# VectorE bound to the order of the source beside the attention units, and a pass's last maxima carried into the next pass

## The chip, the cores and the metric

The kernel runs on one core of one Trainium2 chip. The time is the device time of one execution in microseconds; the number compared is the median of the runs shown. The profile is one execution taken by the hardware profiler. Engine names: PE is TensorE, PEld its weight loads, DVE is VectorE, ACT is ScalarE, POOL is GpSimd, SP is SyncE, which issues most DMAs.

## The reference, cut to what matters

One layer over 512 query rows of width 512: cross attention to a context of 8192 rows with 16 heads of 64, then a state space block with an MLP, then a mixture of 16 experts. The change lies in the cross attention:

```python
q = (scale * (Q @ Wq + bq)).reshape(bs, q_len, NH, DM)   # Q = layernorm(x): 512 rows
k = (K @ Wk + bk).reshape(bs, kv_len, NH, DM)            # K = V = ctx_1024: 8192 rows
v = (V @ Wv + bv).reshape(bs, kv_len, NH, DM)
qk = jnp.einsum('nlhd,nshd->nhls', q, k)
a = jax.nn.softmax(qk, axis=-1)
o = jnp.einsum('nhls,nshd->nlhd', a, v).reshape(bs, q_len, NH * DM)
return o @ Wo + bo
```

The three stages after it are the same before and after the change; the kernel runs them in `tail`.

## The kernel before

Values are kept as pairs of 16-bit floats, a high and a low part, so that most products are three matmuls and most evictions from PSUM are two: ScalarE writes the high part, and VectorE subtracts to get the low part. The heads are taken in 8 pairs, the pairs in 4 passes of two. The context is cut into 16 chunks of 512 rows (`NCH`).

**The filler.** A generator, `filler`, makes keys, values and row maxima, pass by pass. For each chunk it runs two `kproj_units` (PSUM tile `psk`, evicted to `khl` by L257 and L258), two `vproj_units` (`psv`, evicted to `vs` by L280 and L281), and puts two `smax_units` on the list `side`. A unit of these computes plain scores (`psx`, L297), which ScalarE evicts to `sf` (L302) and VectorE folds into a running maximum `runm` (L308 for the first chunk, L310 after). `pump` takes one unit off `side`; it is called after every second projection unit (every fourth in pass 0). After the last chunk of a pass, a `while side` loop runs the rest of the maxima with no projections between. Then `maxrow_units` reduces `runm` (L317 twice, L318), TensorE transposes the result (`ptm`, L321), ScalarE writes it as a row (`mrow`, L323), and two DMAs place it in `qlm`, an operand of the real scores. Its first half runs at the end of the pass, its second inside the next pass's first chunk. `qproj` makes a pass's queries at its start (24 matmuls `psq`). `pass_weights` stages the next pass's weights through one staging buffer (L169), with the split on ScalarE (L175) and VectorE (L176) one chunk after the DMA is issued.

Each unit yields a planned cost in nanoseconds, and `advance` runs the filler until the sum of these costs has reached a given mark.

**The attention.** A unit is one pair and one half of the queries, and has 32 steps (`NSTEP`). In each step, `scores` runs 8 matmuls into two `pss` banks (L359, L360). ScalarE takes the exponential (L367, in even steps also L369), and VectorE casts (L371, odd steps) and subtracts (L372) to get `phl`. The value matmuls `av` (L389, L392) run two steps later, through the list `pend`. After a unit's last step `unit_end` normalises (L399 to L404) and transposes (`pto`, L410). Between a step's parts the loop calls `advance`, so that passes 1 to 3 of the filler are spread over the first `NFILL` = 380 steps at `rate` nanoseconds each. `LEAD` = 11500 ns of filler run before the first scores. Every second step also takes a turn of `weight_prep`, which loads later stages' weights (`mpf`, two buffers), splits them on VectorE (`mph`, L535 and L536) and stores them. The last unit runs beside the first part of `tail`.

**What sets the order.** TensorE's instructions, from pass 0 of the filler to the end of the unit before the last, are in the order of the source (`manual_schedule` with the set `PE`, L541). The other engines' order is chosen by a scheduler when the program is built, from a model of costs; each engine then executes its own list in that order, and waits where an operand is missing.

Of the kernel before, what the change touches and what calls it, by code (L numbers as in the profile page):

```python
# [8 lines left out]
F16 = mybir.dt.float16  # L9
# [7 lines left out]
P = 128  # L17
# [4 lines left out]
CH = 512  # L22
# [7 lines left out]
NPASS = NPAIR // 2  # L30
NDC = NCH // 2
HQ = NQ // 2
NSTEP = 32
PASSN = 16 * (4 * 2592 + 8 * 406) + 2 * 2592 + 600


@with_exitstack
def perceiver_layer(ctx: ExitStack, tc: tile.TileContext, a: dict, out: bass.AP):
# [78 lines left out]
    def R(es, name, bufs):  # L117
        return es.enter_context(tc.tile_pool(name=name, bufs=bufs, side="right", reuse_waits="tile"))
# [7 lines left out]
    def bank_j(shape, dtype, name):  # L126

        if jn[1]:
            jn[0] += 1
            if jn[0] % 3 == 0:  # L130
                return ps_o.tile(shape, dtype, name=name, tag="po1")
        return ps_j.tile(shape, dtype, name=name, tag="pj")
# [3 lines left out]
    sb2 = R(attn, "a2", 2)  # L136
# [30 lines left out]
    def stage_w(src, n, tag, stage=("wst", 1), bufs=2):  # L167
        st = sb2.tile([P, NC4, n], F32, name=f"wst_{tag}", tag=stage[0], bufs=stage[1])
        nc.sync.dma_start(st, src)  # L169
        return lambda: split_w(st, n, tag, bufs)  # L170
# [8 lines left out]
    def load_w(*x, **k):  # L179
        return stage_w(*x, **k)()  # L180
# [102 lines left out]
        nc.sync.dma_start(v_d[g][c // 2][:, tt : tt + 2], vs)  # L283
        yield 648

    def smax_units(c, qh, kh, runm, wide):

        for q2 in range(2):
            sf = sb3.tile([P, 2, 2, CH], F16, name="sf", bufs=2)
            pss = []  # L290
            for qi in range(2):
                qt = 2 * q2 + qi
                for hh in range(2):
                    s = slice(hh * 64, hh * 64 + 64)
                    pool, tag = (ps_s, "pss") if wide and qi else (ps_x, "px")
                    ps = pool.tile([P, CH], F32, name="psx", tag=tag)
                    nc.tensor.matmul(ps, lhsT=qh[s, qt * P : (qt + 1) * P], rhs=kh[s, 0, :], start=True, stop=True)  # L297
                    pss.append((sf[:, qi, hh, :], ps))
                if wide and not qi:
                    continue  # L300
                for dst, ps in pss:
                    nc.scalar.activation(dst, ps, AF.Copy, scale=1.0 / (8.0 * WS))  # L302
                pss = []
                if not qi:
                    yield 406
            r = runm[:, 2 * q2 : 2 * q2 + 2]
            if c == 0:
                nc.vector.tensor_copy(r, sf)  # L308
            else:
                nc.vector.tensor_tensor(r, r, sf, ALU.max)  # L310
            yield 626 if wide else 406

    def maxrow_units(p, runm):
        qlm = state[p]["q"][1]
        m = sb2.tile([P, 2, 4], F32, name="mx")
        for w in (256, 128):
            nc.vector.tensor_tensor(runm[:, :, :, 0:w], runm[:, :, :, 0:w], runm[:, :, :, w : 2 * w], ALU.max)  # L317
        nc.vector.tensor_reduce(m.rearrange("p h q -> p q h"), runm[:, :, :, 0:128], axis=AX.X, op=ALU.max)  # L318
        yield 0
        pt = bank_j([P, P], F32, "ptm")  # L320
        nc.tensor.transpose(pt[0:8, :], m.rearrange("p h q -> p (h q)"), ident)  # L321
        r = sb2.tile([8, P], F16, name="mrow")
        nc.scalar.activation(r, pt[0:8, :], AF.Copy, bias=PSHIFT, scale=-1.0)  # L323
        for hh in range(2):
            nc.sync.dma_start(
                qlm[64:65, hh, :].rearrange("o (a b) -> o a b", b=P), r[hh * 4 : hh * 4 + 4, :]
            )
        state[p]["ready"] = True
        yield 300
# [91 lines left out]
    def filler():  # L421
        side = []

        def pump():
            while side:
                u = next(side[0], None)
                if u is not None:
                    yield u
                    break
                side.pop(0)  # L430

        def pass_weights(g):
            pr = (2 * g, 2 * g + 1)
            out = []
            for src, n, tag, bufs in (
                (a["Wk"][pr[0]], P, "k", 4), (a["Wk"][pr[1]], P, "k", 4), (a["Wv"][g], 256, "v", 2),
                (a["Wq"][pr[0]], P, "q", 2), (a["Wq"][pr[1]], P, "q", 2),
            ):
                w = stage_w(src, n, tag, bufs=bufs)
                yield None  # L440
                out.append(w())
            yield out[0:2], out[2], out[3:5]

        mr, nw = [], None
        for g in range(NPASS):
            pr = (2 * g, 2 * g + 1)
            if g == 0:
                wk0 = load_w(a["Wk"][0], P, "k", bufs=4)
                nct = ctx_first(0)
                wk = [wk0, load_w(a["Wk"][1], P, "k", ("p32", 3), bufs=4)]  # L450
                wv = load_w(a["Wv"][0], 256, "v", ("p32", 3))
                nc.sync.dma_start(x_sb, a["x"])
                wq = [load_w(a["Wq"][p], P, "q", ("t2k", 4)) for p in pr]
            else:
                wk, wv, wq = nw
                qh = [qproj(p, w) for p, w in zip(pr, wq)]
                yield 2 * 2592
            runm = [sb2.tile([P, 4, 2, CH], F16, name=f"runm{i}", tag=f"runm{i}", bufs=1) for i in range(2)] if g else None
            ks = [[None] * NCH for _ in pr]
            for c in range(NCH):  # L460
                if c == NCH - 7 and g < NPASS - 1:
                    nws = pass_weights(g + 1)
                if c >= NCH - 7 and g < NPASS - 1:
                    nw = next(nws, None) or nw
                ct = nct
                nxt = g * NCH + c + 1
                if nxt < NPASS * NCH:
                    nct = ctx_first(nxt) if nxt < NCH else ctx_load(nxt % NCH)
                gens = [kproj_units(p, c, ct, wk[i], ks[i]) for i, p in enumerate(pr)]
                gens += [vproj_units(g, c, ct, wv, j) for j in range(2)]  # L470
                k = 0
                for n, gen in enumerate(gens):
                    for u in gen:
                        yield u
                        k += 1
                        if k % (2 if g else 4) == 0:
                            yield from pump()
                    if mr and c == 0:
                        yield from mr.pop(0)
                if g == 0 and c == 0:  # L480
                    first_norm()
                    qh = [qproj(p, w) for p, w in zip(pr, wq)]
                    yield 2 * 2592
                    runm = [sb2.tile([P, 4, 2, CH], F16, name=f"runm{i}", tag=f"runm{i}", bufs=1) for i in range(2)]
                if c == 2:
                    for p, q in zip(pr, qh):
                        qplace(p, *q)
                side += [smax_units(c, qh[i][0], ks[i][c], runm[i], g == 0) for i in range(2)]
            while side:
                yield from pump()  # L490
            mr = [maxrow_units(p, runm[i]) for i, p in enumerate(pr)]
            for x in mr:
                yield next(x)
            if g == NPASS - 1:
                for x in mr:
                    yield from x
            passes[0] = g + 1

    fill = filler()
    done = [0.0]  # L500

# [3 lines left out]
            done[0] = 1e12 if u is None else done[0] + u  # L505

    PE = {mybir.EngineType.PE}

    def weight_prep():
        zero = sb2.tile([P, 2 * DM], F16, name="zero", tag="t2k", bufs=4)  # L510
# [29 lines left out]
    ms = ExitStack()  # L540
    ms.enter_context(tc.manual_schedule(engines=PE))  # L541

    units = [(p, h) for p in range(NPAIR) for h in range(2)]
    NLAST = len(units) - 1
    LEAD = 11500
    loads = {}

    def load(j):
        if j < len(units) * NDC:
            loads[j] = main_load(units[j // NDC][0], j % NDC)  # L550
# [2 lines left out]
        advance(done[0] + 1)  # L553
    jn[1] = False
    start = done[0]
    load(0)
    advance(start + LEAD)
    load(1)
    pend, enders, early = [], [], weight_prep()
    NFILL = 12 * NSTEP - 4  # L560
    rate = (NPASS - 1) * PASSN / NFILL
    sp = (sb2, sb3, 3)
    po = []

# [10 lines left out]
    for n in range(NLAST * NSTEP):  # L575
# [3 lines left out]
        if m % 4 == 0 and n:  # L579
            load(n // 4 + 1)  # L580
        cur = scores(u, m, loads[n // 4], sp, n > NFILL)
        advance(start + LEAD + (n + 0.5) * rate)
        if enders and m == 4:
            for _ in enders.pop(0):
                pass
        while len(pend) > (2 if m == 2 else 1):
            drain()
        advance(start + LEAD + (n + 1.0) * rate)
        pend.append((u, m, cur))
        if n < NFILL and n % 2 == 0:  # L590
            next(early, None)
# [4 lines left out]
    while enders:  # L596
        for _ in enders.pop(0):
            pass
    attn.close()
    ms.close()  # L600
    late2 = R(late, "late2", 1)
    sp = (late2, late2, 3)
# [756 lines left out]
```

## Time and profile before

| what | us |
|---|---|
| median of 3 runs | 2649.29 (2645.43 to 2654.56) |
| profiled execution, device time | 2653.45 |
| its span, first to last instruction | 2651.7 |
| TensorE busy | 2410.6 |
| VectorE busy | 2049.4 |
| ScalarE busy | 1955.5 |
| mean granted TensorE clock | 0.959 |

Pass 0 of the filler runs alone until about 265 us; attention and filler run together from about 280 to 1625 us; attention alone to about 1810 us; the last unit with the beginning of the tail to about 1915 us; then the tail. Lines such as L372 are line numbers of the kernel before. Matmuls overlap, and their ends are modelled, so TensorE's busy time is more than the time its matmuls need; the distance between their starts and the granted clock tell more.

### The profile page before, as it was taken

To read this page: it belongs to the slowest core of one execution; us is meant where nothing else is said; L and a number is where in the kernel's file an instruction comes from. 1 tells how busy PE (TensorE), PEld (TensorE's weight loads), DVE (VectorE), ACT (ScalarE), POOL (GpSimd) and SP (SyncE) were. 2 spreads that over 40 slices of the span, in tenths; PEclk is the share of its full clock that TensorE was granted. 3 is DMA by queue.
4 is the path that set the end of the run, shared out by engine and by line. 5 is a ranking of instruction groups with operands and counts; after the bars stand their busy time and mean duration, and the time that the engine had idled before them with its cause. 6 is when DMAs were issued, how large, how long until landed. Compare 5 with 4: busy or idle time off the path is not lost. (4 is left out here: it accounts for less than half of the span.)

```text
span 2651.7 us, 54346 instructions
## 1 busy us (share of the span) xinstructions
PE 2410.6 (91%) x21806; PEld 1693.5 (64%) x21806; DVE 2049.4 (77%) x2403; ACT 1955.5 (74%) x3734; POOL 44.2 (2%) x58
## 2 busy tenths in 40 slices
PE   7999998999999899998999998998878688998895
PEld 4454676777666677766677766997656466665442
DVE  6876688877877877777877777997899999633785
ACT  5787787888787788867788887997868476432784
POOL 2000000000000000000000000000000000001001
PEclk9999999999899999989999998999989889999998
DMA  7973899866598866658966655887511322675896
GB/s 265 308 255 128 268 284 270 242 169 187 166 268 264 265 189 176 184 152 250 253 176 190 173 162 129 201 204 206 171 56 41 96 72 82 229 233 200 294 337 222
DMA packets 353686, 531.42 MB, mean 200 GB/s; under 512 B 25106, under 2 KB 218834, under 8 KB 353300
## 3 DMA queue, kind: packets, MB, share of 16 engines
q1 hardware_dynamic: 352148, 523.69, 65.6%
q0 software_dynamic: 1280, 4.20, 0.5%
q8 instruction: 173, 2.83, 0.5%
q14 instruction: 85, 0.70, 0.1%
HBM read 397.68 MB, written 126.94 MB: 198 GB/s over the span
## 5 line engine op out<-in xcount | busy, mean ns | idle before, releaser
L372 DVE TENSOR_TENSOR phl<-p,phl 128x1024 f16<-128x1024 f32 x512 | 625.9, 1224 | 175.0 <-ACT phl L369 158.9
L367 ACT ACTIVATE p<-pss 128x512 f32<-128x512 f32 x1024 | 596.8, 619 | 126.1 <-PE pss L360 50.7
L302 ACT ACTIVATE sf<-psx 128x512 f16<-128x512 f32 x1024 | 557.7, 622 | 79.1 <-PE psx L297 77.2
L359 PE MATMUL pss<-qhh,k 128*128 128x256 f16 x2048 | 486.2, 277 | 18.5 <-ACT phl L369 18.0
L360 PE MATMUL pss<-qlm,kb 128*128 128x256 f16 x2048 | 485.2, 276 | 0.6 <-DMA kb<-k_d 0.4
L389 PE MATMUL po<-v,phl 128*128 128x130 f16 x4096 | 327.2, 222 | 5.2 <-DVE oq L402 4.7
L310 DVE TENSOR_TENSOR runm<-runm,sf 128x2048 f16<-128x2048 f16 x240 | 292.4, 1218 | 45.7 <-ACT sf L302 45.2
L389 PEld LDWEIGHTS <-phl 128*128 128x128 f16 x4096 | 273.9, 99 | 69.4 <-issue 21.5
L369 ACT ACTIVATE phl<-pss 128x512 f16<-128x512 f32 x512 | 312.3, 610 | 0.0
L274 PE MATMUL psv<-wh_v,ctxc 128*128 128x256 f16 x1024 | 283.4, 277 | 7.7 <-DVE khl L258 3.4
L275 PE MATMUL psv<-wl_v,ctxc 128*128 128x256 f16 x1024 | 282.2, 276 | 1.2 <-DVE wl_v L176 1.2
L276 PE MATMUL psv<-wh_v,ctxc 128*128 128x256 f16 x1024 | 282.1, 276 | 0.0
L359 PEld LDWEIGHTS <-k 128*128 128x128 f16 x2048 | 202.2, 99 | 63.7 <-issue 18.0
L360 PEld LDWEIGHTS <-kb 128*128 128x128 f16 x2048 | 202.7, 99 | 61.0 <-issue 22.2
L297 PE MATMUL psx<-khl,qh 64*128 64x512 f16 x1024 | 212.5, 395 | 21.3 <-ACT sf L302 18.4
L371 DVE CAST phl<-p 128x1024 f16<-128x1024 f32 x256 | 176.1, 688 | 58.1 <-ACT p L367 57.7
L392 PE MATMUL po<-v,phl 128*128 128x65 f16 x4096 | 209.9, 194 | 9.3 <-DVE phl L372 9.3
L250 PE MATMUL psk<-ctxc,wh_k 128*128 128x512 f16 x512 | 198.6, 388 | 21.1 <-DVE vs L281 10.5
L919 PE MATMUL py<-hs,ident 128*128 128x256 f32 x512 | 148.1, 447 | 67.1 <-DVE hs L916 67.0
L251 PE MATMUL psk<-ctxc,wh_k 128*128 128x512 f16 x512 | 197.2, 385 | 0.7 <-DVE ctxc L234 0.7
L252 PE MATMUL psk<-ctxc,wl_k 128*128 128x512 f16 x512 | 196.8, 384 | 0.0
L392 PEld LDWEIGHTS <-phl 128*128 128x128 f16 x4096 | 172.8, 98 | 12.8 <-DVE phl L372 12.0
(304 smaller groups left out, 3711.9 us busy)
## 6 DMA issues: line engine op xcount, KB each, us to landing
v<-v_d SPq DMA_DIRECT2D x128, 520.0 KB, 4.4
k<-k_d SPq DMA_DIRECT2D x256, 256.0 KB, 5.8
ctxc<-ctx_d SPq DMA_DIRECT2D x96, 512.0 KB, 5.2
wef<-in_gu_dram SPq DMA_DIRECT2D x72, 512.0 KB, 5.9
v_d<-vs SPq DMA_DIRECT2D x128, 260.0 KB, 3.8
k_d<-khl SPq DMA_DIRECT2D x128, 256.0 KB, 4.2
kb<-k_d SPq DMA_DIRECT2D x128, 256.0 KB, 5.4
wpm<-w_d SPq DMA_DIRECT2D x48, 512.0 KB, 3.9
```

The lines of the kernel that those rows point to most:

```text
L274: nc.tensor.matmul(ps[:, t, :], lhsT=ct[i // 2][:, 0, i % 2, sl], rhs=wh[:, i, :], start=i == 0, stop=False)
L275: nc.tensor.matmul(ps[:, t, :], lhsT=ct[i // 2][:, 0, i % 2, sl], rhs=wl[:, i, :], start=False, stop=False)
L276: nc.tensor.matmul(ps[:, t, :], lhsT=ct[i // 2][:, 1, i % 2, sl], rhs=wh[:, i, :], start=False, stop=i == NC4 - 1)
L302: nc.scalar.activation(dst, ps, AF.Copy, scale=1.0 / (8.0 * WS))
L310: nc.vector.tensor_tensor(r, r, sf, ALU.max)
L359: nc.tensor.matmul(ps[:, hh], lhsT=k[:, hh, sl], rhs=qhh[:, hh, qs], start=True, stop=False)
L360: nc.tensor.matmul(ps[:, hh], lhsT=b[:, hh, sl], rhs=qlm[:, hh, qs], start=False, stop=True)
L367: nc.scalar.activation(p32[:, i], pss[i], AF.Exp, scale=sc)
L369: nc.scalar.activation(ph[:, i], pss[i], AF.Exp, scale=sc)
L372: nc.vector.tensor_tensor(pl, p32, ph, ALU.subtract)
L389: nc.tensor.matmul(o, lhsT=ph[:, i, hh, qs], rhs=vv, start=first, stop=False, **kw)
L392: nc.tensor.matmul(o, lhsT=pl[:, i, hh, qs], rhs=vv_, start=False, stop=last, **kw)
```

## The change

VectorE is added to the engines that keep the order of the source, and this begins where the filler's first pass has been made, ahead of the first loads of keys; until there TensorE alone keeps it, as before. ScalarE, SyncE and GpSimd keep the scheduler's order. The loop at the end of a pass goes, except in the last pass. The last chunk's maxima stay on `side`, the two `maxrow_units` are put behind them, and both run inside the next pass's first chunks, with a pump after every projection unit as long as `side` holds more than two. `maxrow_units` has three turns of no planned cost between the reduce and the transpose. `runm` is made when the first chunk's maxima run. In the last pass, every unit of the rest has 800 ns of planned cost added (`LAST / 10`). `LEAD` goes from 11500 to 27500, `NFILL` from 380 to 378, and `rate` takes both into account.

```diff
+LAST = 8000
...
-    def smax_units(c, qh, kh, runm, wide):
+    def smax_units(c, i, qh, kh, runm, wide):
+        if c == 0:
+            runm[i] = sb2.tile([P, 4, 2, CH], F16, name=f"runm{i}", tag=f"runm{i}", bufs=1)
...
-            r = runm[:, 2 * q2 : 2 * q2 + 2]
+            r = runm[i][:, 2 * q2 : 2 * q2 + 2]
...
-    def maxrow_units(p, runm):
+    def maxrow_units(p, i, runm):
+        runm = runm[i]
...
-        yield 0
+        for _ in range(3):
+            yield 0
...
-                        if k % (2 if g else 4) == 0:
+                        if k % (2 if g else 4) == 0 or len(side) > 2:
                             yield from pump()
-                    if mr and c == 0:
-                        yield from mr.pop(0)
...
-                side += [smax_units(c, qh[i][0], ks[i][c], runm[i], g == 0) for i in range(2)]
-            while side:
-                yield from pump()
-            mr = [maxrow_units(p, runm[i]) for i, p in enumerate(pr)]
-            for x in mr:
-                yield next(x)
+                side += [smax_units(c, i, qh[i][0], ks[i][c], runm, g == 0) for i in range(2)]
+            side += [maxrow_units(p, i, runm) for i, p in enumerate(pr)]
             if g == NPASS - 1:
-                for x in mr:
-                    yield from x
+                while side:
+                    yield from pump()
+                    yield LAST / 10
...
     PE = {mybir.EngineType.PE}
+    ALL = PE | {mybir.EngineType.DVE}
...
-    LEAD = 11500
+    LEAD = 27500
...
     start = done[0]
+    ma = ExitStack()
+    ma.enter_context(tc.manual_schedule(engines=ALL))
     load(0)
...
-    NFILL = 12 * NSTEP - 4
-    rate = (NPASS - 1) * PASSN / NFILL
+    NFILL = 12 * NSTEP - 6
+    rate = ((NPASS - 1) * PASSN + LAST - LEAD) / NFILL
...
     attn.close()
+    ma.close()
     ms.close()
```

More of the change, by code (lines that the diff above doesn't have):

```diff
@@ L442, in pass_weights @@
             yield out[0:2], out[2], out[3:5]
-        mr, nw = [], None
+        nw = None
         for g in range(NPASS):
@@ L457, in filler @@
                 yield 2 * 2592
-            runm = [sb2.tile([P, 4, 2, CH], F16, name=f"runm{i}", tag=f"runm{i}", bufs=1) for i in range(2)] if g else None
+            runm = [None, None]
             ks = [[None] * NCH for _ in pr]
@@ L483, in filler @@
                     yield 2 * 2592
-                    runm = [sb2.tile([P, 4, 2, CH], F16, name=f"runm{i}", tag=f"runm{i}", bufs=1) for i in range(2)]
                 if c == 2:
```

## The prediction

> **What bounds the kernel now.** I read the page first, its busy times and its 40 slices:
>
> ```profile
> PE 2410.6 (91%) x21806; PEld 1693.5 (64%) x21806; DVE 2049.4 (77%) x2403; ACT 1955.5 (74%) x3734; POOL 44.2 (2%) x58
> ...
> PE   7999998999999899998999998998878688998895
> ...
> PEclk9999999999899999989999998999989889999998
> ```
>
> TensorE is the busiest, and its dents stand beside dents of its granted clock. So I then cut the attention stage (240 to 1650 us) into a table of stretches; columns are busy us and instruction count per engine, the granted clock, DMA share and GB/s.
>
> ```profile
> 395.00:425.00 30.00, 23.52 (x217) 16.07 (x215) 23.70 (x38) 17.19 (x35) 0.00 (x0) 0.83 0.87 259
> 675.00:705.00 30.00, 25.57 (x185) 14.08 (x183) 24.28 (x26) 21.27 (x41) 0.00 (x0) 0.77 0.37 109
> 855.00:890.00 35.00, 26.15 (x253) 18.63 (x251) 27.73 (x43) 19.92 (x41) 0.00 (x0) 0.90 0.81 254
> 1600.00:1650.00 50.00, 40.71 (x435) 30.63 (x434) 38.68 (x38) 37.30 (x74) 2.19 (x5) 0.83 0.43 108
> 900.00:1140.00 240.00, 239.91 (x2519) 174.37 (x2517) 182.47 (x202) 204.51 (x402) 0.00 (x0) 1.00 0.68 191
> ```
>
> The last row is the stage undisturbed: TensorE full, clock 1.00, 10.50 matmuls per us, about 3.36 us per attention step (it holds 72 of the subtracts L372, one a step). Nothing but TensorE's own work bounds it, and the change leaves that work as it is. The other rows are holes, of two kinds.
>
> First kind: a weight split (mph, L535) at the head of VectorE's queue, waiting for its DMA. The timeline of VectorE, then of TensorE:
>
> ```profile
> 398.99 0.74 DVE L258 SCALAR_TENSOR_TENSOR khl<-psk,bk_sb,khl 128x512 f16<-128x512 f32 x1
> 403.17 0.76 DVE L535 TENSOR_SCALAR mph<-mpf 128x512 f16<-128x512 f32 x2 [3.44 <-DMA mpf<-in_outp_dram]
> ...
> 409.06 0.68 DVE L281 TENSOR_TENSOR vs<-psv,vs 128x512 f16<-128x512 f32 x1
> ```
>
> ```profile
> 409.80 0.69 PE L410 MATMUL pto<-ident,oq 128*128 128x128 f32 x2 [6.47 <-DVE vs L281]
> ```
>
> The vs eviction that frees TensorE's PSUM bank stands behind the waiting split and behind what piled up, and TensorE idles 6.47 us. The waits of 260 to 1560 us show it as a class (total, times, longest):
>
> ```profile
> PE psk L250 <- DVE vs L281: 10.5, 2, 6.7
> PE pto L410 <- DVE vs L281: 10.2, 3, 6.5
> ```
>
> ```profile
> DVE phl L372 <- ACT phl L369: 134.4, 110, 3.7
> DVE phl L371 <- ACT p L367: 54.4, 73, 2.9
> DVE mph L535 <- DMA mpf<-in_w_dram: 24.2, 12, 5.4
> DVE mph L535 <- DMA mpf<-in_Wo_dram: 11.1, 4, 4.4
> DVE mph L535 <- DMA mpf<-in_rsu_dram: 10.8, 3, 5.7
> ```
>
> Second kind: at each pass's end the loop drains its last maxima alone. The timeline of TensorE at 680 us:
>
> ```profile
> 679.77 0.27 PE L359 MATMUL pss<-qhh,k 128*128 128x256 f16 x1
> 679.88 0.27 PE L360 MATMUL pss<-qlm,kb 128*128 128x256 f16 x1
> ...
> 682.20 0.86 PE L297 MATMUL psx<-khl,qh 64*128 64x512 f16 x2 [1.08 <-ACT sf L302]
> ...
> 685.18 1.07 PE L297 MATMUL psx<-khl,qh 64*128 64x512 f16 x2 [0.99 <-ACT sf L302]
> 686.18 0.40 PE L359 MATMUL pss<-qhh,k 128*128 128x256 f16 x1
> ...
> 689.86 1.07 PE L297 MATMUL psx<-khl,qh 64*128 64x512 f16 x2 [1.25 <-ACT sf L302]
> ```
>
> Each psx pair waits for ScalarE's evictions, the clock goes to half, and the scores, which started every 0.11 us at 679.8, are recorded at 0.40.
>
> [...] The clock: from the rows, the stretch 675 to 705 has a granted clock of 0.77, and no recorded wait there is over 1.3 us. [...] I take the row: many short gaps cost the clock too.
>
> [...] But in 900 to 1140 us weight loads are at 174/240 = 73% and 256-column matmuls start back to back every 0.11 us; there is no more to be had from TensorE there. [...]
>
> **Size of the holes.** First kind, by missing matmuls at 10.50 per us: 395-425: (315 - 217)/10.5 = 9.3 us. In the same way 745-760 (124 matmuls) 3.2, 795-830 (288) 7.6, 855-890 10.9, 1205-1240 (261) 10.1, 1265-1315 (463) 5.9: together 47 us. Second kind, idle plus clock loss: 240-280 (busy 37.15, clock 0.87) 2.9 + 5.2 = 8; 675-705: 11; 1140-1175 (30.80, 0.80) 4.2 + 7.0 = 11; 1600-1650: 9.3 + 8.5 = 18: together 48 us. So 95 us can be had at most.
>
> **The change, part by part.**
>
> *Source order on VectorE.* In the source a mpf fetch is issued four steps of the preparation ahead of its split, one every two attention steps: 8 x 3.36 = 27 us, against waits of at most 5.7 us. In the built order the fetches on SP stand about every 12 instructions instead of in bunches, and the splits one pair at a time among the attention steps. The 57 us of VectorE waits on mpf should go, and with them the 47 us. Residue for late stores or loads on SP: 5 us.
>
> What it adds: VectorE now stands where something is late. Its work is the same, 77%. The built order of ScalarE follows TensorE's in both kernels, so VectorE's operations become ready in about the order they stand in. Behind a waiting subtract (L372) queue khl, vs and running maxima; waiting for those are TensorE's next psk/psv bank (two banks, a group every 6.5 us: four per chunk, eight steps per chunk) and the av matmuls, which run two steps after their scores (pend). A lag of some 4 us is covered; the waits in the rows are 134.4/110 = 1.2 us. Bounds: 0, and the rival below; I take 6 us.
>
> *Next pass's weights.* Split by ScalarE (L175) then VectorE (L176), now one per chunk, on one staging buffer: a DMA starts when the split before it is done, and ScalarE's half stands only about three steps later. In the trace the longest such wait of ScalarE is 6.29 us (wh_q at 815 us), 12.4 us in all. Bounds 0 and 12; I take 6.
>
> *Drain removed.* An eviction costs ScalarE 0.51 us (four sf in a row take 2.05 in its timeline), a psx pair TensorE about 0.21. Pass 0: four last units of four evictions (2.05 us of ScalarE) each beside one kproj unit: 2.05 + 0.16 of ScalarE against 0.65 + 0.85 of TensorE, 0.7 us each, 3 us. Passes 1 and 2: each half unit gives ScalarE 1.02 us beside a 0.65 us projection; at 1.67 of them a step (1.76 us of planned filler over 0.648 + 0.406) ScalarE needs 1.70 + 3 x 0.51 + 0.25 = 3.5 us against TensorE's 3.36, 1 us over five steps. The maxrow operations (1.22 + 0.69 + 1.22 us, twice a pass) are a lump in VectorE's order, mostly inside its lag: 2 us. So 3 us per pass, 6. The four pumps between reduce and transpose hide the reduce. Last pass: with 800 ns added per unit there are 1.43 half units a step, ScalarE 1.53 + 1.46 = 3.0 us against TensorE's 2.2 us (1.6 a step without filler, 1650 to 1810 us: 2356 matmuls, 24 a step; and 0.6): 0.8 x 5.6 steps = 4.5, with the maxima 6 us. Together 15 us of the 48 stay.
>
> *LEAD, LAST, NFILL.* The same filler, 16 us of it ahead of the first scores: 0, as TensorE is full in both places. The maxima's rows (two qlm DMAs each) go out later, behind the zero fills and ahead of the first k loads on SP; the longer lead covers them. The last ones come about six steps before the unit that needs them: some 10 us against a 4 us landing. POOL's order is unchanged.
>
> **Sum.** 95 - 5 - 6 - 6 - 15 = 63 us. From the profiled execution's 2653.45: 2590; its time is 4.2 us over the median, so on the scale of the median 2649.29 - 63 = 2586.
>
> **Rivals.** (1) *All comes back*: no new waits, a residue of 10 us: 2564. For it: undisturbed stretches of 240 us exist. Against it: ScalarE at 85% there leaves little room at the pass ends.
> (2) *Half comes back*: ScalarE, whose order stays the scheduler's, takes the weight waits at full price (12), every maxima lump falls on TensorE (8 x 2.9 = 23), and short gaps keep costing the clock: gain some 30, 2620.
> (3) *Slower: VectorE becomes the bound.* It is free for about 23% of a 3.36 us step, 0.75 us. If waits in its fixed order pass that per step, every step grows. Now 110 of some 390 steps wait 1.2 us; if all did, 0.45 us over, times 378 steps = 170 us, less the 63 gained: 107 slower; at 1.05 us a step, 0.30 x 378 = 113, or 50 slower: 2700. It decides from 0.92 us a step. Against it: the order of ScalarE agrees with VectorE's new one.
> (4) *The order is not what bound*, holes elsewhere take their place: no change, 2649.
>
> **How the numbers follow.** Case of the sum 0.56 (2572 to 2604), (1) 0.12, (2) 0.14, (4) 0.05, (3) 0.13. A change within 0.3%, 8 us, cannot be told from none. Faster 0.82, same 0.05, slower 0.13. The range 2558 to 2641 takes in (2) and most of (1), and leaves (3), (4) out.
>
> **What would show it.** Right: no mph wait on mpf over 2 us; no clock below 0.9 in a 30 us stretch between 300 and 1560 us; VectorE still near 2049 us busy; the tail from the end of attention as long as now. Wrong: psk, psv or po waiting on VectorE in every step, with L372 waits in most steps (rival 3); sf or wh waits with half clock at the pass ends (rival 2).

## The result, and the profile after

The changed kernel takes 2610.67 us (median, 2607.52 to 2615.35, four runs) against 2649.67 us for the kernel before, measured beside it: ratio 0.9854, 95% interval 0.9831 to 0.9877, or 39 us faster. The forecast was 2586 us, a gain of 63. The direction and the first half of the mechanism were right; the gain was 24 us too high.

The page of the profile after, with its busy times and two rows of its slices (TensorE and its granted clock):

```profile
PE 2392.4 (92%) x21806; PEld 1684.3 (64%) x21806; DVE 2063.4 (79%) x2403; ACT 1948.3 (75%) x3734; POOL 44.3 (2%) x58
...
PE   7999899999999999999999998998877688998995
...
PEclk9999999999999999999999999999989899999997
```

The dents that the clock row of before has in its first 25 slices are gone at this resolution. The attention stage in stretches (columns as before: length, busy us and count of TensorE, weight loads, VectorE, ScalarE, GpSimd; clock, DMA share, GB/s):

```profile
395.00:425.00 30.00, 30.00 (x320) 21.61 (x317) 26.46 (x38) 25.34 (x53) 0.00 (x0) 1.00 0.74 213
...
855.00:890.00 35.00, 34.45 (x352) 24.47 (x351) 29.62 (x39) 29.34 (x60) 0.00 (x0) 1.00 0.80 230
...
1145.00:1180.00 35.00, 29.96 (x282) 21.49 (x280) 26.93 (x32) 20.52 (x42) 0.00 (x0) 0.90 0.68 183
1200.00:1540.00 340.00, 337.00 (x3539) 246.59 (x3536) 273.61 (x319) 287.34 (x568) 0.00 (x0) 1.00 0.73 209
1560.00:1610.00 50.00, 40.98 (x468) 32.49 (x466) 39.09 (x40) 37.74 (x76) 2.65 (x5) 0.90 0.44 118
```

The holes of the first kind (395, 855) are full, and 340 us run on end at 10.4 matmuls per us, against 10.50 in the undisturbed stretch before. What is left stands at the pass ends: 1145 to 1180, and above all the last one, 1560 to 1610, idle for 9.0 of its 50 us, where 1600 to 1650 had 9.3 before, at a clock of 0.90 instead of 0.83. TensorE's waits from 260 to 1560 us, total, times, longest:

```profile
PE psx L300 <- ACT sf L305: 7.4, 10, 2.5
PE ptm L326 <- DVE vs L282: 6.0, 3, 2.7
PE ptm L326 <- DVE mx L322: 4.2, 2, 2.6
PE ptm L326 <- DVE khl L259: 3.2, 1, 3.2
```

Three of the four are new: TensorE at the transpose of the maxima (`ptm`). And VectorE's own waits in the same stretch:

```profile
DVE phl L377 <- ACT phl L374: 165.4, 167, 2.7
DVE phl L376 <- ACT p L372: 32.8, 45, 1.9
DVE vs L282 <- ACT vs L281: 14.4, 19, 3.1
```

No `mph` wait is in that list any more. (The lines of the kernel after are shifted: L377 is L372 of before, L322 is L318, L326 is L321, L282 is L281, L259 is L258, L305 is L302.)

To place gains in time, the next table gives the start of the n-th attention step in each trace, as the difference in us to the same step before (278.5 us for step 0, 506.3, 1205.3, 1548.0, 1809.8 and 2651.7 for the end). (Left out of it: steps 32, 128 and 384, told below where they matter.) The changed kernel puts 16 us more filler ahead of step 0, which comes back by step 378. The last column is the median time of the runs; the kernel before had a median of 2649.6 to 2650.4 each time. A trace is one of the runs and need not be the median one: that of the order alone without the last maxima is the fastest of its five (2568.66 us).

| kernel | step 0 | 64 | 256 | 352 | 480 | end | median us |
|---|---|---|---|---|---|---|---|
| changed kernel | +14.8 | +4.2 | -22.0 | -39.1 | -41.7 | -38.0 | 2610.67 |
| order alone | -1.0 | -12.6 | -22.5 | -38.7 | -34.8 | -35.4 | 2618.28 |
| carrying alone | +12.8 | +13.8 | -12.4 | -27.2 | -32.0 | -34.5 | 2621.86 |
| before, no load waits | +4.4 | +1.7 | -15.8 | -26.0 | -25.1 | -22.7 | 2630.05 |
| carrying alone, no load waits | +10.4 | +2.3 | -33.4 | -46.5 | -49.9 | -53.0 | 2601.93 |
| changed, eight turns | +9.6 | -1.6 | -35.6 | -47.8 | -52.0 | -52.4 | 2602.14 |
| order alone, last maxima left out | -13.8 | -25.4 | -54.2 | -69.9 | -81.8 | -84.7 | 2575.45 |
| changed, eight turns, last maxima left out | +8.6 | +1.1 | -30.2 | -46.9 | -66.7 | -69.2 | 2586.58 |

All kernels in the table have their gain by step 480; the tail gives or takes a few us at most.

### The profile page after: what moved, and what is told of

Same layout as the page of the kernel before. It is cut to its first block, busy times and chain, and to the rows that moved or that the text cites. A ratio compares the mean times of both kernels' runs of the same rounds, so it can differ in the third digit from the quotient of the medians.

```text
span 2613.6 us, 54412 instructions
## 1 busy us (share of the span) xinstructions
PE 2392.4 (92%) x21806; PEld 1684.3 (64%) x21806; DVE 2063.4 (79%) x2403; ACT 1948.3 (75%) x3734; POOL 44.3 (2%) x58
## 5 line engine op out<-in xcount | busy, mean ns | idle before, releaser
L377 DVE TENSOR_TENSOR phl<-p,phl 128x1024 f16<-128x1024 f32 x512 | 626.7, 1225 | 189.4 <-ACT phl L374 177.6
L372 ACT ACTIVATE p<-pss 128x512 f32<-128x512 f32 x1024 | 597.8, 621 | 113.4 <-issue 41.9
L305 ACT ACTIVATE sf<-psx 128x512 f16<-128x512 f32 x1024 | 559.1, 627 | 69.2 <-PE psx L300 68.6
L364 PE MATMUL pss<-qhh,k 128*128 128x256 f16 x2048 | 482.7, 275 | 15.0 <-ACT phl L374 12.4
L394 PEld LDWEIGHTS <-phl 128*128 128x128 f16 x4096 | 271.8, 98 | 61.7 <-issue 14.6
L922 PEld LDWEIGHTS py<-hs,ident 128*128 128x128 f32 x512 | 107.8, 219 | 105.5 <-DVE hs L919 85.2
```

The lines of the kernel that those rows point to most:

```text
L364: nc.tensor.matmul(ps[:, hh], lhsT=k[:, hh, sl], rhs=qhh[:, hh, qs], start=True, stop=False)
L372: nc.scalar.activation(p32[:, i], pss[i], AF.Exp, scale=sc)
L377: nc.vector.tensor_tensor(pl, p32, ph, ALU.subtract)
L394: nc.tensor.matmul(o, lhsT=ph[:, i, hh, qs], rhs=vv, start=first, stop=False, **kw)
L922: nc.tensor.matmul(py[:, j, :], lhsT=ident, rhs=hs[:, n, 1:], start=k == 0, stop=False)
```

## The experiments

**One half of the change at a time.** First the order alone, on the kernel before:

```diff
     PE = {mybir.EngineType.PE}
+    ALL = PE | {mybir.EngineType.DVE}
...
     start = done[0]
+    ma = ExitStack()
+    ma.enter_context(tc.manual_schedule(engines=ALL))
...
     attn.close()
+    ma.close()
```

> The kernel before with one part of the change: VectorE keeps the order of the source from the same point on; the pass ends, LEAD, NFILL and the rate are those of before. Theory (two separate gains: the order takes away the holes behind waiting weight splits, the carry those at the pass ends): no mph wait on mpf over 2 us, the drains at 250, 680, 1150 and 1600 us stay at half clock, gain about 30 us, 2620. Rival A (the carry alone brings the gain): within 8 us of 2649. Rival B (the order is only of use together with the carry): slower than 2657.

Measured: 2618.28 us (2617.37 to 2621.67), ratio 0.9885 (0.9864 to 0.9906). No `mph` wait is left. From step 288 to 352, where nothing disturbs either kernel, before takes 216.4 us and this one 216.5: the fixed order of VectorE costs nothing there. The pass ends are as empty as they were: from 240 to 280 us TensorE is busy for 37.15 us at a granted clock of 0.87 in both kernels, and at 684.55 us the scores start every 0.21 us, as from 686.18 us on before.

Then carrying alone: the changed kernel with VectorE left to the scheduler.

```diff
-    ALL = PE | {mybir.EngineType.DVE}
+    ALL = PE
```

> The changed kernel with VectorE's order given back to the scheduler: carry, LEAD, LAST and NFILL stay. Theory (two separate gains): the mph waits on mpf are back (some 50 us of VectorE), the long half-clock stretches at the pass ends are not; gain about 12 to 17 us, 2635. Rival A (the carry alone brings the gain): about 2611, as the whole change. Rival B (order and carry only work together): 2649 or slower.

Measured: 2621.86 us (2618.87 to 2624.81), ratio 0.9898 (0.9879 to 0.9917): 28 us, well over the 12 to 17 expected. The load waits are there (VectorE's waits, 250 to 1560 us):

```profile
DVE mph L535 <- DMA mpf<-in_w_dram: 21.4, 13, 4.0
DVE mph L535 <- DMA mpf<-in_outp_dram: 9.0, 3, 3.6
DVE mph L535 <- DMA mpf<-in_rsd_dram: 5.0, 3, 2.0
DVE mph L535 <- DMA mpf<-in_inp_dram: 4.7, 2, 3.0
```

So the order gives 31 us and carrying 28, but together they give 39, not 59. Twenty us had to be found.

**The load waits by themselves.** On the kernel before, `mpf` is fetched once and used for all blocks, so that no split has a load to wait for (later stages get wrong weights):

```diff
+        kept = []
         def fetch(j):
+            if kept:
+                return kept[0]
...
+            kept.append(f)
             return f
```

> The kernel before, with the weight preparation fetching only its first block and splitting it again and again: every later mpf fetch is left out, so the stages after attention get wrong weights. VectorE's operations and the stores stay, the scheduler still orders VectorE. Theory (the first kind of hole is the wait for the DMA at the head of VectorE's queue): nearly all of the 47 us come back though no order is kept, about 2605 to 2612. Rival (the hole is the bunching of the splits ahead of vs and the subtracts, the wait only a part): under half, 2630 or more.

Measured: 2630.05 us (2628.88 to 2631.03), ratio 0.9925 (0.9901 to 0.9950): 20 us, where the rival begins (2630 or more): the wait is only a part of the hole. Two thirds of what the order gives by step 352 (26.0 of 38.7) come with the waits. What is left is the built order, which stays, with its bunched splits and the waits for stores that come in. Of VectorE's waits here and of TensorE's timeline, one line each:

```profile
DVE mph L540 <- DMA w_d<-mph: 6.8, 5, 2.8
```

```profile
413.36 0.44 PE L410 MATMUL pto<-ident,oq 128*128 128x128 f32 x2 [3.75 <-DVE vs L281]
```

The splits now wait in part for the store of their buffer's last content, and the hole at 400 us remains although nothing waits for a load: from 403.4 to 413 us VectorE works without a pause, and the eviction stands behind its splits and subtracts. Steps 32 to 64, which hold that hole, take 119.3 us before, 116.3 here, 108.4 with the order alone, 111.1 with carrying alone, 106.8 with both. Each half closes most of it, and it can only be closed once: 10.9 and 8.2 us apart, 12.5 together, so about 7 of the 20 us.

The same edit on carrying alone:

> The version that carries the maxima but leaves VectorE to the scheduler (2621.86 us), with mpf fetched once and used for every block, so that the splits have no load to wait for; later stages get wrong weights by it. Carrying alone gained 28 us and the order alone 31, but both together 39. If that is because the version with carrying alone has lost part of the first kind already (its built order is another one, and TensorE's longest waits for VectorE are 3.4 and 5.4 us instead of 6.7 and 6.5), taking the load waits away gives it no more than 11 us, down to about 2611 us or above. If the waits still cost it what they cost the kernel before (20 us), it comes to about 2602 us, below the changed kernel, and the two gains overlap for some other reason.

Measured: 2601.93 us (2595.65 to 2609.45), ratio 0.9820 (0.9793 to 0.9847). The 11 us I expected at most were wrong: the load waits cost this version the same 20 us as before, and 20 + 28 add up to the 48 measured. So load waits and carrying look independent, within the scatter of this run. And this kernel, with the scheduler's order, beats the changed kernel by 9 us: the source order must bring a cost of its own once the maxima are carried.

**What the order costs at the pass ends.** The timeline of VectorE after, at the end of the third pass, then that of TensorE:

```profile
1153.37 1.94 DVE L321 TENSOR_TENSOR runm<-runm 128x2048 f16<-128x2048 f16 x2
1155.35 1.22 DVE L322 TENSOR_REDUCE mx<-runm 128x8 f32<-128x1024 f16 x1
1156.48 0.68 DVE L376 CAST phl<-p 128x1024 f16<-128x1024 f32 x1
1157.20 1.23 DVE L377 TENSOR_TENSOR phl<-p,phl 128x1024 f16<-128x1024 f32 x1
1158.34 0.68 DVE L282 TENSOR_TENSOR vs<-psv,vs 128x512 f16<-128x512 f32 x1
...
1166.78 1.95 DVE L321 TENSOR_TENSOR runm<-runm 128x2048 f16<-128x2048 f16 x2
1168.76 1.22 DVE L322 TENSOR_REDUCE mx<-runm 128x8 f32<-128x1024 f16 x1
```

```profile
1159.08 0.27 PE L326 MATMUL ptm<-ident,mx 128*8 128x128 f32 x1 [2.39 <-DVE vs L282]
...
1170.04 0.31 PE L326 MATMUL ptm<-ident,mx 128*8 128x128 f32 x1 [2.65 <-DVE mx L322]
```

The folds and the reduce are 3.2 us in one piece. The first transpose waits for the eviction behind them, which frees its bank; the second waits for the reduce itself. The six transposes up to 1560 us wait 13.4 us in all (the three rows of `ptm` above), the last pass's two another 5.7 (two of the recorded texts below say 15.9 for the six). In the version with carrying alone the waits of the six are at most 1.7 us each. Putting more turns between reduce and transpose tests it:

```diff
-        for _ in range(3):
+        for _ in range(8):
             yield 0
```

> The changed kernel with eight turns of no planned cost between reduce and transpose in maxrow_units instead of three. Theory (the transposes ptm come too early: in the trace of the change they stand 1.7 to 3.8 us for mx or for an eviction queued behind the reduces, six of them 15.9 us in all): these waits go in passes 1 and 2 and shrink in the last, gain 8 to 14 us on the change, about 2599. Rival (the reduces are a lump in VectorE's order, and the next psk or psv bank waits for the same lump instead): within 4 us of 2611.

Measured: 2602.14 us (2600.16 to 2604.86), ratio 0.9823 (0.9801 to 0.9844). It beats both kernels, the changed one by 8.5 us. The transpose's waits, 260 to 1560 us, are down to:

```profile
PE ptm L326 <- DVE vs L282: 1.7, 2, 1.2
```

The mean granted clock from 240 to 1650 us says the same. The rows of the kernel before, of the changed kernel and of this one, in this order:

```profile
240.00:1650.00 1410.00, 1347.76 (x13577) 961.85 (x13576) 1085.71 (x1299) 1126.26 (x2202) 2.29 (x6) 0.97 0.72 208
```

```profile
240.00:1650.00 1410.00, 1368.21 (x14196) 990.97 (x14195) 1136.81 (x1346) 1159.20 (x2282) 2.75 (x6) 0.99 0.74 215
```

```profile
240.00:1650.00 1410.00, 1371.88 (x14359) 996.77 (x14358) 1146.76 (x1355) 1170.38 (x2304) 2.75 (x6) 1.00 0.74 216
```

**Four variants of that version, none of them better.** ScalarE kept to the source order too:

```diff
-    ALL = PE | {mybir.EngineType.DVE}
+    ALL = PE | {mybir.EngineType.DVE, mybir.EngineType.Activation}
```

> The kernel with eight turns, and ScalarE put into the order of the source as well. Theory (ScalarE's built order already follows TensorE's, so binding it changes next to nothing; only the waits of wh on its weight DMA, 5.6 us in the trace of the change, may go): within 5 us of that kernel's 2602, rather below. Rival (the scattered holes of some 20 us between 500 and 1450 us come from ScalarE being placed by the scheduler's model): 2590 or less. Rival (in the source a split or an eviction stands where ScalarE must wait): 2610 or more.

2601.47 us (2595.50 to 2606.20): no difference. The last pass's last maxima put on the list after two projection units of its last chunk, instead of after the chunk:

```diff
+                last = g == NPASS - 1 and c == NCH - 1
...
+                    if last and n == 2:
+                        side += [smax_units(c, i, qh[i][0], ks[i][c], runm, g == 0) for i in range(2)]
...
-                        if k % (2 if g else 4) == 0 or len(side) > 2:
+                        if k % (2 if g else 4) == 0 or len(side) > 2 or last:
...
-                side += [smax_units(c, i, qh[i][0], ks[i][c], runm, g == 0) for i in range(2)]
+                if not last:
+                    side += [smax_units(c, i, qh[i][0], ks[i][c], runm, g == 0) for i in range(2)]
```

> The kernel with eight turns; in the last pass alone, the last chunk's smax units are put on the list after its two kproj units and taken after every vproj unit, so that they run beside projections and not beside attention alone. Theory (the last pass's end is bound by ScalarE: eight half units of 1.02 us in steps in which ScalarE has 1.53 of 1.6 us used): gain 5 to 8 us on 2602, about 2596, and the hole at 1560 to 1600 us goes. Rival (the maxima rows and their reduces set that end): within 3 us of 2602.

2603.19 us (2600.66 to 2606.00): no gain. The last scores ended 6 us sooner, and steps 384 and 480 stood where they had. The reduce cut into pieces, with a turn after each fold and six turns after it:

```diff
         for w in (256, 128):
             nc.vector.tensor_tensor(runm[:, :, :, 0:w], runm[:, :, :, 0:w], runm[:, :, :, w : 2 * w], ALU.max)
+            yield 0
...
-        for _ in range(8):
+        for _ in range(6):
```

> The kernel with eight turns, and a turn after each of the two folds in maxrow_units (six turns after the reduce), so that the 3.2 us lump of VectorE becomes three pieces of 1.2 us at most with subtracts between. Theory (with the transposes moved away the lump is covered by the two-step slack of the value matmuls and the banks): gain under 4 us, 2600. Rival (the lump still stops a bank's eviction at each pass end): gain 6 to 10 us, 2594.

2602.95 us (2597.40 to 2605.18): nothing. And both of these together:

> Last maxima early and reduce in pieces together. Theory: the sum of the two gains, about 2594. Rival (both give back the same wait): no better than the better one.

2602.18 us (2600.11 to 2603.45): no gain in the time. In its profile, though, step 480 stands at -58.0, 6 us ahead of the eight turns alone, and the tail gives it back (848.7 us from step 480 to the end instead of 841.4). Why the tail is longer was not tried.

**What the drains were worth.** In three kernels the maxima of each pass's last chunk are left out, so that a pass ends with none to make, only with the reduce and the transposes: the order alone, the changed kernel, and the changed kernel with eight turns.

```diff
-                side += [smax_units(c, i, qh[i][0], ks[i][c], runm, g == 0) for i in range(2)]
+                if c < NCH - 1:
+                    side += [smax_units(c, i, qh[i][0], ks[i][c], runm, g == 0) for i in range(2)]
```

What falls away with them is eight units of eight matmuls, 32 pairs (the first text below counts them too high, its 14 us are right). Their own price is read in an undisturbed stretch of the timeline before:

```profile
906.70 0.27 PE L275 MATMUL psv<-wl_v,ctxc 128*128 128x256 f16 x1
906.81 0.27 PE L276 MATMUL psv<-wh_v,ctxc 128*128 128x256 f16 x1
907.01 0.39 PE L297 MATMUL psx<-khl,qh 64*128 64x512 f16 x2
907.34 0.63 PE L389 MATMUL po<-v,phl 128*128 128x130 f16 x8
```

From the last `psv` to the `po` behind the pair it is 0.53 us instead of the 0.11 us from one `psv` to the next, so a pair costs 0.42 us, and 32 of them 13.4 us. (That is 0.21 us for 512 columns over 64 rows; three `psk` matmuls of 512 columns over 128 rows take 0.65 us there, from 911.36 to 912.01 us, so 0.22 each. This is the half rate of the first text below. The prediction writes 0.21 us for a pair; its sums take 0.42.)

> The kernel before with VectorE in the order of the source (as in the run of the order alone, 2618.28 us), and with the maxima of each pass's last chunk left out, so that the row maxima lack one chunk in four: nothing is left to drain at the end of a pass. If the drains were worth the 48 us of the prediction, this run takes those and the scores' own matmuls that are left out, 8 units of 8 pairs of half-rate score matmuls, some 14 us: 2618 - 62 = about 2556 us. If the 48 us counted the scores' own work and the half clock twice, as the attention step table suggests (about 20 to 25 us of true loss), it is 2618 - 14 - 22 = about 2582 us.

Measured: 2575.45 us (2568.66 to 2588.08), ratio 0.9731 (0.9705 to 0.9757). Against the order alone that is 42.8 us; less 13.4 for the scores' own work, 29 us went with the maxima, not 48. The run is not quite without a drain. The reduce at the end of the last pass still holds up its two transposes (TensorE's waits, 250 to 1550 us; in the order alone this is 6.4 us):

```profile
PE ptm L321 <- DVE mx L318: 9.6, 2, 6.8
```

> The changed kernel with the maxima of each pass's last chunk left out in the same way. What it gains on the changed kernel (2610.67 us) is the scores' own work, some 14 us, and what the carried maxima still cost. If carrying hides the drains all but for the six waits of TensorE for the transposes' inputs (15.9 us in the profile after): 2611 - 14 - 16 = about 2581 us, as fast as the order alone without those maxima. If the prediction's term of 15 us was right and something else is late, it stays above 2590 us.

Measured: 2577.29 us (2576.43 to 2589.36, three runs near 2577 and two near 2588), ratio 0.9734 (0.9711 to 0.9758). That is 33.4 us under the changed kernel; less the scores' own 13.4, the carried maxima still cost it 20 us. And it is 1.8 us from the order alone without those maxima, measured beside it.

> The changed kernel with eight turns between reduce and transpose (2602.14 us) and with the maxima of each pass's last chunk left out. The run of the order alone without those maxima still has two waits of the transpose for its reduce (9.6 us), so its 2575.45 us is not yet a kernel without drains; this one should have neither. If nothing but the scores' own 13.8 us is left in the version with eight turns, it comes to 2602 - 14 = 2588 us, which cannot be, as the runs without those maxima are at 2575 and 2577 already: so some 11 us or more is still lost at its pass ends. If the waits for the reduce are all that those two runs still have, this is about 2577 - 8 = 2569 us, and the drains of the order alone were 2618 - 14 - 2569 = 35 us. If the transposes cost nothing there, it stays at 2577 us, and they were 29 us.

Measured: 2586.58 us (2584.22 to 2588.95), ratio 0.9757 (0.9736 to 0.9779). This is the value that the text called impossible: 2602.14 less 13.4 is 2588.7. With eight turns the carried maxima cost their own work and 2 us. The reason I held it impossible was the median of the run before it, whose two groups lie 11 us apart. The one trace kept of that run belongs to the slower group (2589.36 us), and in the attention it agrees with this one (step 480 at -65.2 and -66.7). What the faster group does otherwise no trace shows, so the difference of the two medians isn't read as an effect of the turns.

This kernel is 11 us slower than the order alone without those maxima (15 us by step 480, in a trace 7 us under its median). The same comparison with three turns gave 1.8 us. If the 11 us are real, they come from the other differences: the larger `LEAD`, `NFILL` with its `rate`, the 800 ns in the last pass's rest, the rule of a pump after every unit, or where the reduce runs. None of them was tried alone, and runs of one of these kernels lie up to 20 us apart.

## Why the prediction was right or wrong, point by point

Along the medians the gain of 39.0 us is 31.4 for the order, + 29.4 for the drains, - 21.8 that did not come. Each is a difference of runs of the section above. The missing 21.8 divide in two ways. With the changed kernel's own run without last maxima they are 20.0 of drain left in it (2610.67 - 2577.29 - 13.4) and 1.8 between the kernels without last maxima. With the run of eight turns they are 10.7 (2610.67 - 2586.58 - 13.4) and 11.1. The profiles at step 480 give 34.8 + 33.6 - 26.7 = 41.7, the same picture. The runs without last maxima scatter by up to 20 us, so the terms are good to some 5 to 10 us, and which division holds is open.

The forecast was 24 us too high, and the term at fault is that of the pass ends: 48 - 15 = 33 us there, of which 29.4 - 21.8 = 7.6 came on top of the order. The drains were taken for 48 instead of 29.4 (18.6 us), and what stays of them for 15 instead of 21.8 (6.8 us); the first kind gave 1.4 more than forecast.

- **The first kind: right.** 47, less 5, 6 and 6 for its residues, is 30; the order alone gave 31.4. Why it holds TensorE up was right in outline (20 us go with the load waits alone). Some 11 us more came from the built order with no load at fault, which the 47 had put down to the loads, and none of the three residues was found at its size where the prediction put it. That the sums agree so closely is in part luck.
- **In-order waits, 6 us: right in sum, wrong in place.** In undisturbed steps they cost nothing (64 steps take 216.4 us without the order and 216.5 with it), though the waits of `phl` for ScalarE grew in number from 110 to 158 with the order alone and to 167 in the changed kernel. At the pass ends they cost 8.5 us, which the eight turns give back.
- **Weight waits of ScalarE, 6 us: unmeasured as a cost.** From 260 to 1560 us ScalarE waits 2.9 and 2.7 us for `wst` after, and 8.0 before (the prediction's 12.4 also counts waits ahead of 260 us). Giving ScalarE the source order moved nothing.
- **"Second kind: together 48 us": too high.** 29 us went with the maxima (33.6 by step 480), and even with all 9.6 us of the last reduce it stays under 48. The prediction charged every idle microsecond and every loss of clock in those stretches to the drain (its 11 us at 675 to 705 are 30 - 25.57 = 4.4 of idle and 0.23 x 30 = 6.9 of clock). Leaving the maxima out of the order alone brought the first step after each pass (0, 128, 256, 384) forward by 9, 7, 5 and 11 us beyond the scores' own work, where the prediction had 8, 11, 11 and 18: part of what was lost there did not go with the maxima. What that part is was not isolated.
- **Residue of the drains, 15 us: 10.7 or 20.0, by the run taken, and wrong in its parts.** "The four pumps between reduce and transpose hide the reduce" is a step that failed. They pass in less time than VectorE needs to reach and finish a 3.2 us lump: six transposes wait 13.4 us. Eight turns bring that to 1.7 and the time down by 8.5 us.
- **"*LEAD, LAST, NFILL* ... 0": open.** Between the kernels without last maxima 1.8 us (three turns) or 11.1 us (eight) are left for these and the new pumping rule.
- **The marks.** Three held: no `mph` wait on a load; VectorE 2063.4 us busy on the same 2403 instructions; the tail within 4 us of before. The clock mark held only for stretches set every 30 us from 300 us on (0.94 at least). Set across the end of the third pass, 30 us fall under its 0.9 (the row below the list). So it pointed at the place where the gain was short. A wait on `ptm` should have been a mark too.
- **The rivals.** VectorE did not become the bound. Of the case *half comes back* (2620 us) one part was true, the lump of the maxima falling on TensorE, with some half clock beside it (0.50 from 1160 to 1162 us, inside the same row); its weight waits at full price were not seen. The changed kernel lies between that case and the sum.

```profile
1144.00:1174.00 30.00, 24.96 (x239) 18.47 (x237) 23.50 (x27) 16.77 (x34) 0.00 (x0) 0.89 0.69 186
```

Two readings of the rows held. The prediction saw no more to be had from TensorE in 900 to 1140 us, at 10.50 matmuls per us with weight loads at 73%; with the holes closed, 1200 to 1540 us run the same way, at 10.4 matmuls per us with weight loads at 246.59 / 340 = 73% and the clock at 1.00. And the clock did fall beside short gaps (the rows are in the last section). One reading was off: the scores in the drain are not 0.40 us apart, which is their recorded length (0.27 at 679.8 us), but 0.21 us, twice the 0.11:

```profile
686.18 0.40 PE L359 MATMUL pss<-qhh,k 128*128 128x256 f16 x1
686.37 0.42 PE L360 MATMUL pss<-qlm,kb 128*128 128x256 f16 x1
686.59 0.42 PE L359 MATMUL pss<-qhh,k 128*128 128x256 f16 x1
```

## What to carry to other kernels

Here a split at the head of VectorE's queue that waited for its transfer (5.7 us at most) held up the evictions behind it, and so TensorE's banks (6.7 us at most): taking the load waits away gave 20 us, and an order that the builder keeps, with each load well ahead of its use and the splits spread out, 31. Binding a queue to the source order also binds every long piece of work in it: place the consumer of a 3 us lump by the time the queue needs to reach and pass it (eight turns instead of three, 8.5 us). Size a hole by a run that takes its cause away, since idle time and lost clock in the stretches (48 us) were 1.6 times what went with the cause (29 us), and two cures of one hole don't add (31 and 28 us gave 39).

## What the runs showed of the hardware

Here the clock halved where TensorE had only short gaps. In the kernel before, the stretch from 684 us on in steps of 2 us (the granted clock is the third column from the end):

```profile
684.00:686.00 2.00, 0.90 (x4) 0.09 (x1) 2.00 (x3) 2.00 (x4) 0.00 (x0) 0.88 0.98 295
686.00:688.00 2.00, 2.00 (x9) 1.04 (x8) 1.05 (x1) 1.53 (x4) 0.00 (x0) 0.50 0.93 224
...
696.00:698.00 2.00, 2.00 (x10) 1.26 (x9) 2.00 (x2) 1.37 (x4) 0.00 (x0) 0.50 0.00 0
```

The clock is at 0.50 from 686 to 698 us, and TensorE's longest recorded wait there is 1.25 us. What in these gaps lowers the clock no run shows. Over 240 to 1650 us the mean clock rose from 0.97 to 0.99 with the change and to 1.00 with eight turns; 0.03 of 1410 us is some 42 us of TensorE's time at full clock (an estimate, 28 to 49 with the rounding of the rows), beside 48 us that this version gains in all. In the same rows its busy time grows by 24 us. The two overlap, since the mean clock takes in idle time as well; so about half of the gain is idle time, and about half is clock (an estimate from these rows).
